# Pooling the first pair's expert tokens by gathering eight rows from a DRAM table

## Chip, cores, metric

The kernel runs on one core of one Trainium2 chip. The metric is the device time of one execution in microseconds. All arithmetic is in float32.

## The reference, cut to what matters

The input is 4 images of 128 channels by 64 x 64, so 4 x 4096 tokens of 128 numbers. Layer 0 adds a full softmax attention between the tokens of an image. Layer 1 adds a running attention with 8 heads to the tokens and then a mixture of 64 experts that choose tokens. This last part is where the change lies:

```
logits = einsum('bsd,ed->bse', x, gate_w) + gate_b     # x: normalised tokens
probs  = softmax(logits, axis=1)                       # over the 4096 tokens
vals, idx = top_k(probs.transpose(0, 2, 1), 8)         # 8 tokens per image and expert
gathered = take_along_axis(x, idx)
pooled   = einsum('bked,bke->bed', gathered, topv)     # weighted sum of the 8 tokens
h   = gelu([pooled, 1] @ weight1);  out = [h, 1] @ weight2
outputs[b, idx] += topv * out                          # back to the 8 tokens
```

## The kernel before

`t` holds all tokens on the chip, 128 tokens by 128 numbers a chunk, four chunks to a block of 512 tokens, 32 blocks in all (8 to an image). Layer 0 runs first and takes the first 1440 us. Then `layer1` runs `loop()` (L1146): one turn n per block, 0 to 31, with the order of PE written out by hand (`tc.manual_schedule`), while a scheduler orders DVE, ACT, POOL (GpSimd) and SP from data dependences and from the `tc.issue_after` pins.

A turn n does this on PE, in this order: the first four key matmuls of block n + 1 (`keys`, L364); the transposes of the score exponentials (`weights`, L910); the transposes of the normalised tokens of block n - 2 for the gate (`gate_turn`, L1036); four more key matmuls; the values (`values`, L946, sixteen records); the gate's logits of block n - 2 (`gate_logits`, L1044); the transposes of the tokens of block n + 2 (`turned`, L354); the running sums (`totals`, L962); the scores of block n + 1 (`score`, L839); the outputs (`outputs`, L985 and L992).

The scores go through `scan`: DVE copies them (L853), takes the running maximum (L858) and subtracts it (L862); ACT takes the exponential (L866); POOL copies the last maximum into `state` (L867) and the exponentials into `es` (L871); DVE sums them (L879) and takes the reciprocal (L884). `spread` sends the reciprocals through DRAM (`rd`) and back, broadcast, as `rb` (L892, L899, on SP's queue). POOL multiplies the exponentials with a mask into `em` (L925), and DVE multiplies `em` with `rb` (L934); `outputs` reads it.

The gate normalises block n - 1 in turn n (`gate_norm`): DVE makes the statistics and the root's reciprocal `grs` (L92), POOL normalises the four chunks into `gate_room` (L96) and copies the roots (L1030). `gate_logits` writes the logits into `lgs[p]`, where p is a pair of images, 0 or 1, and the 128 partitions are 2 images x 64 experts; DVE keeps the eight largest logits of each block in `cand[p]` (L1051).

Once the first pair's 16 blocks have logits, `k0 = n - 18` counts its eight columns of blocks. In turn 18 `select(0)` takes the eight largest logits of the row, `top`, from `cand`. In turns 18 to 25 `pick_exp` (ACT, L1090) and `pick_keep` (DVE, L1100) replace the logits by the exponentials where the logit is at least the eighth largest, and by zero elsewhere. In turns 19 to 26 the pooling follows as dense products: `pick_turn` transposes four chunks of this sparse array on PE (L1111), DVE multiplies them with the roots (`ct`, L1114), and `pick_add` multiplies them with all 1024 tokens of the two blocks on PE (`pick_sum`, L1125) and adds the result to `total` (L1134, L1136). `pick_turn` is pinned ahead of DVE's `weighted` (L934). `total` is used in the tail by `pool_tokens`, which subtracts its mean and divides. The second pair is pooled the same way in the tail, after the loop.

A test at the end counts how many tokens each expert chose (`count`, by ACT's sign function). When a row has more than eight, or a layer 0 sum is out of range, both layers run again in a safer form (`ready` false).

Of the kernel before, what the change touches and what calls it, by code (L numbers as in the profile page):

```python
# [18 lines left out]
def conv_attn_hybrid_kernel(  # L19
# [23 lines left out]
    nc = tc.nc  # L43
    B, C, N = x.shape
    R = w1t.shape[1]
    NH = qt.shape[1]
    E = gwt.shape[1]
# [3 lines left out]
    BLK = 512  # L51
    NBLK = N // BLK
    CPB = BLK // P
# [258 lines left out]
    rows = resid.tile([P, B * NCH], F32, tag="rows", name="rows")  # L312
# [475 lines left out]
    def layer1(pre, ready):  # L788
# [6 lines left out]
        with ExitStack() as kept, ExitStack() as l1:  # L795
# [5 lines left out]
            lgp = pool("lg", side="right")  # L801
            gp = pool("gate", side="right")
# [201 lines left out]
            cand = [lgp.tile([P, NBLK, 8], F32, tag=f"ca{p}", name=f"{pre}ca_{p}") for p in range(B // 2)]  # L1004
            den = lgp.tile([P, B // 2, NBLK], F32, tag="den", name=f"{pre}den")

            count = lgp.tile([P, B // 2, NBLK], F32, tag="count", name=f"{pre}count")
            rden = lgp.tile([P, B // 2], F32, tag="rden", name=f"{pre}rden")

            total = lgp.tile([P, C], F32, tag="total", name=f"{pre}total")  # L1010

            gate_room = gp.tile([P, 2 * BLK], F32, tag="gate_room", name=f"{pre}gate_room")
            gmv, grs, xgs, gate_xts, picks, eighth, cts, lefts = {}, {}, {}, {}, {}, {}, {}, {}

            def gate_stats(n):
                gmv[n] = gp.tile([P, CPB, 2], F32, tag="gmv", name=f"{pre}gmv_{n}", bufs=2)
# [3 lines left out]
            def gate_norm(n, engine):  # L1020
                grs[n] = gp.tile([P, CPB], F32, tag="grs", name=f"{pre}grs_{n}", bufs=2)
                root = roots(grs[n], gmv[n])
                xgs[n] = gate_room[:, :BLK].rearrange("p (c d) -> p c d", c=CPB)
                for c in range(CPB):
                    normalise(
                        engine, xgs[n][:, c, :], n * CPB + c, gmv[n][:, c, 0:1],
                        grs[n][:, c : c + 1],
                    )

                nc.gpsimd.tensor_copy(rs1[:, bass.ts(n, CPB)], grs[n])  # L1030
                return root
# [21 lines left out]
            def select(p):  # L1053

                flat = cand[p].rearrange("p k e -> p (k e)")
                top = gp.tile([P, 8], F32, tag=f"top{p}", name=f"{pre}top_{p}")
                nc.vector.max(out=top, in_=flat)
                ng = gp.tile([P, 1], F32, tag=f"ng{p}", name=f"{pre}ng_{p}")
                i = nc.vector.tensor_scalar_mul(ng, top[:, 0:1], -1.0)
                picks[p], eighth[p] = ng, top[:, 7:8]  # L1060
# [13 lines left out]
                i = nc.vector.tensor_add(flat, flat, sel)  # L1074
                return i.ins
# [54 lines left out]
            def pick_add(p, k):  # L1130
# [4 lines left out]
                else:  # L1135
                    nc.vector.tensor_add(total, total, pp)  # L1136

            def divisors(p):
                nc.vector.tensor_reduce(rden[:, p : p + 1], den[:, p, :], AX.X, ALU.add)
                nc.vector.reciprocal(rden[:, p : p + 1], rden[:, p : p + 1])  # L1140
# [5 lines left out]
            def loop():  # L1146
# [8 lines left out]
                for n in range(NB):  # L1155
# [23 lines left out]
                    with ExitStack() as order:  # L1179
                        if k0 == 0:  # L1180
                            with tc.issue_after(made[2][1]):
                                order.enter_context(tc.issue_after(select(0)))
                        if 0 <= k0 < NBLK:
                            left = gp.tile([P, BLK], F32, tag="left", name=f"{pre}left_0_{k0}")
                            marked = pick_mark(0, k0, left)
                            if marked is not None:
                                order.enter_context(tc.issue_after(marked))
                        if 1 <= k0 <= NBLK:
                            order.enter_context(tc.issue_after(pick_turn(0, k0 - 1, ps_kv)))
                        if k0 == NBLK:  # L1190
                            divisors(0)
                        aas = weighted(ems, rbs)
# [5 lines left out]
                    vs, last = values(n, xt_of[n])  # L1198
                    if n >= 2:
                        best = gate_logits(n - 2, ps_kv)  # L1200
                    if 1 <= k0 <= NBLK:
                        pick_add(0, k0 - 1)
                    with tc.issue_after(last):
                        if n >= 1 and more:
# [11 lines left out]
                    if more:  # L1216
# [360 lines left out]
```

## Time and profile before

| | |
|---|---|
| median of 3 runs (lowest to highest) | 2379.5 us (2378.95 to 2381.96) |
| profiled execution, its own time | 2380.49 us |
| its span, first to last instruction | 2378.7 us |
| TensorE clock granted | 0.997 of full speed |
| PE busy | 2338.3 us, 98% |
| DVE, ACT, POOL busy | 1495.5, 1205.3, 302.9 us |
| L1111, dense transposes, both pairs | 64 records, 10.7 us busy |
| L1125, dense products, both pairs | 256 records, 18.2 us busy |
| L1114, `ct` on DVE, both pairs | 16, 11.0 us busy |
| transfers issued from POOL | none |

A timeline row gives start and duration in microseconds, the engine, the line, the operation, output and inputs by their names, their shapes and how many instructions were merged; a bracket tells how long the engine had stood idle before it and what ended that. PE is TensorE's matmul, PEld its weight load, SPq SyncE's queue. A float32 product leaves two matmul records, a transpose one. An idle engine costs nothing unless what it does next is waited for.

### The profile page before, as it was taken

What the parts mean: (1) busy time and instruction counts of PE and PEld (TensorE: products, weight loads), DVE (VectorE), ACT (ScalarE), POOL (GpSimd) and SP (SyncE); (2) the same over time, 40 slices, a digit from 0 to 9 for tenths busy, and PEclk for the clock granted to TensorE, in tenths of its full rate; (3) what the DMA queues carried; (4) which work ended last, traced back from release to release, by engine and by line L of the source; (5) the groups of instructions that cost most, each with busy time, mean ns of one, the idle gap of its engine ahead of it and who ended that gap; (6) DMA issues with size and microseconds to landing.
All of it is one profiled execution on the core that took longest, in us unless ns stands there. A gap on an engine that the chain in (4) does not pass through costs nothing.

```text
span 2378.7 us, 45711 instructions
## 1 busy us (share of the span) xinstructions
PE 2338.3 (98%) x19416; PEld 1554.5 (65%) x19416; DVE 1495.5 (63%) x2593; ACT 1205.3 (51%) x1637; POOL 302.9 (13%) x338
## 2 busy tenths in 40 slices
PE   7999999999999999999999999999999999999997
PEld 3477777677778677778777775555555555655554
DVE  6666666666656666655555556666666676776655
ACT  5444444444444444443433435666666666666541
POOL 0000000000000000000000001343333343333300
PEclk9999999999999999999999999999999999999999
DMA  3200110001100000020000000212112112112388
GB/s 83 75 23 19 44 37 1 17 13 23 49 25 1 19 12 23 16 54 1 1 1 1 1 1 19 55 38 51 43 38 56 38 44 49 38 38 52 122 307 323
DMA packets 61766, 109.94 MB, mean 46 GB/s; under 512 B 10096, under 2 KB 35184, under 8 KB 61552
## 3 DMA queue, kind: packets, MB, share of 16 engines
q1 hardware_dynamic: 57824, 101.22, 14.9%
q10 hardware_dynamic: 3728, 5.71, 0.7%
q8 instruction: 154, 2.52, 0.5%
q14 instruction: 60, 0.49, 0.1%
HBM read 85.40 MB, written 8.91 MB: 40 GB/s over the span
## 4 chain that ended last, share of the span: by engine, by line


## 5 line engine op out<-in xcount | busy, mean ns | idle before, releaser
L608 PE MATMUL av<-pr,am 64*128 64x512 f32 x4096 | 1057.5, 591 | 0.3 <-ACT pr L587 0.3
L587 ACT ACTIVATE pr<-sc 128x1024 f32<-128x1024 f32 x512 | 523.8, 1023 | 674.5 <-PE sc L583 605.8
L590 DVE TENSOR_TENSOR acc<-acc,pr 128x1024 f32<-128x1024 f32 x480 | 586.9, 1223 | 436.1 <-ACT pr L587 436.0
L608 PEld LDWEIGHTS av<-pr,am 64*128 64x128 f32 x4096 | 634.3, 187 | 260.8 <-issue 40.8
L583 PE MATMUL sc<-e,e 64*128 64x512 f32 x2048 | 617.7, 592 | 1.9 <-DMA e<-ee 1.9
L583 PEld LDWEIGHTS sc<-e,e 64*128 64x128 f32 x2048 | 316.8, 187 | 106.0 <-issue 17.8
L364 PE MATMUL pk<-room,wks 128*128 128x512 f32 x508 | 238.3, 607 | 2.2 <-ACT room L365 1.9
L946 PE MATMUL pv<-wvs,room 128*128 128x512 f32 x512 | 225.4, 593 | 0.5 <-ACT room L365 0.4
L950 ACT ACTIVATE v<-pv 128x512 f32<-128x512 f32 x256 | 152.7, 597 | 72.0 <-PE pv L946 72.0
L934 DVE TENSOR_TENSOR em<-em,rb 128x1024 f32<-128x1024 f32 x64 | 78.4, 1224 | 153.4 <-DMA rb<-rd 153.4
L365 ACT ACTIVATE room<-pk 128x512 f32<-128x512 f32 x254 | 146.8, 597 | 54.5 <-PE pk L364 54.2
L828 POOL MEMSET ew<- 128x1024 f32 x1 | 1.0, 952 | 1360.8 <-PE av L608 1360.8
L946 PEld LDWEIGHTS pv<-wvs,room 128*128 128x128 f32 x512 | 96.3, 190 | 119.1 <-issue 113.7
L364 PEld LDWEIGHTS pk<-room,wks 128*128 128x128 f32 x508 | 89.4, 189 | 107.8 <-issue 79.0
L925 POOL TENSOR_TENSOR em<-et,mask 128x1024 f32<-128x1024 f32 x64 | 122.6, 1936 | 81.3 <-ACT et L912 81.3
L985 PEld LDWEIGHTS po<-v,em 64*64 64x64 f32 x4096 | 113.7, 134 | 28.1 <-DVE before L972 25.1
L96 POOL TENSOR_SCALAR gate_room<-t,gmv,grs 128x128 f32<-128x128 f32 x120 | 95.2, 805 | 281.8 <-DVE grs L92 193.7
L985 PE MATMUL po<-v,em 64*64 64x128 f32 x4096 | 122.3, 273 | 1.8 <-issue 1.8
L884 DVE RECIPROCAL rr<-rr 128x512 f32<-128x512 f32 x32 | 107.3, 3353 | 1.1
L866 ACT ACT_TABLE_LOAD x24 | 30.8, 1283 | 115.8 <-DVE ss L862 115.8
L972 DVE TENSOR_TENSOR before<-before,pt 128x128 f32<-128x128 f32 x256 | 72.7, 284 | 9.7 <-PE pt L962 3.8
L879 DVE TENSOR_TENSOR_SCAN rr<-ones,state,ss 128x512 f32<-128x512 f32 x28 | 42.0, 1500 | 46.6 <-ACT ss L866 46.6
(208 smaller groups left out, 2029.5 us busy)
## 6 DMA issues: line engine op xcount, KB each, us to landing
rb<-rd SPq DMA_DIRECT2D x128, 256.0 KB
fw<-in_fw_dram SPq DMA_DIRECT2D x39, 512.0 KB
room<-in_fw_dram SPq DMA_DIRECT2D x18, 512.0 KB
t<-in_xtok_dram SPq DMA_DIRECT2D x32, 256.0 KB
e<-ee SPq DMA_DIRECT2D x63, 128.0 KB
x<-in_x_dram SPq DMA_DIRECT2D x12, 512.0 KB
e<-ee SPq DMA_DIRECT2D x63, 64.0 KB
out_dram<-t SPq DMA_DIRECT2D x8, 256.0 KB
```

Of the source, the lines that this page charges most:

```text
L96: i = engine.tensor_scalar(out=dst, in0=t[:, chunk, :], scalar1=mean, scalar2=rs, op0=ALU.subtract, op1=ALU.mult)
L364: nc.tensor.matmul(pk, wks[:, h, :], xt, start=True, stop=True)
L365: nc.scalar.activation(kss[h], pk, AF.Silu)
L583: nc.tensor.matmul(sc[:, u, :], e2[halves[u], p, :], e1[halves[u], :], start=True, stop=True)
L587: nc.scalar.activation(pr, sc, AF.Exp)
L590: added.append(nc.vector.tensor_add(acc, acc, pr).ins)
L608: nc.tensor.matmul(av, am[h, j, :], pr[h, u, :], start=(j == 0), stop=(j == NCH - 1))
L884: inverse = nc.vector.reciprocal(rr, rr).ins
L925: nc.gpsimd.tensor_tensor(em, eq.unsqueeze(2).to_broadcast([P, 2 * NH, H2]), mask.unsqueeze(1).to_broadcast([P, 2 * NH, H2]), ALU.mult,)
L946: nc.tensor.matmul(pv.rearrange("p h d -> p (h d)"), xt[:, bass.ts(2 * q + s, P)], wvs[:, bass.ts(m, BLK)], start=True, stop=True,)
L950: last = nc.scalar.activation(v[:, bass.ts(m, HPB), :], pv, AF.Silu).ins
L985: nc.tensor.matmul(po[s * H2 : (s + 1) * H2, u, q, :], aas[q][half, s, h, :], vs[2 * q + s][half, h, :], start=(q == 0 and h == 0), stop=F ...
```

## The change

It acts on the first pair only, and only in the normal run (`ready` true). Each block that `gate_norm` normalises in turns 1 to 16 is also written from `gate_room` to a table `xd` in DRAM, 8192 rows of 128 numbers, by a transfer issued from POOL. In turns 18 to 25 `find` takes, on DVE, the positions of the block column's eight candidates within the block and turns them into row numbers of `xd` (`where`). In turn 26 `gather_chosen` picks, for each of the row's eight largest logits, the row number of the candidate that equals it, and POOL issues eight indirect transfers of 128 rows each from `xd`; equal logits among the eight raise `count` by 100, which makes the end test fail. ACT takes the eight exponentials as `share`. In turn 27 `sum_chosen` adds the eight gathered tokens, each times its share, into `total`. `pick_turn` and `pick_add` are no longer called for the first pair. `pick_exp` and `pick_keep` stay.

```diff
-            count = lgp.tile([P, B // 2, NBLK], F32, tag="count", name=f"{pre}count")
+            count = lgp.tile([P, B // 2, NBLK + 1], F32, tag="count", name=f"{pre}count")
...
+            PAIR = 2 * N
+            if ready:
+                xd = dram.tile([PAIR, C], F32, tag="xd", name=f"{pre}xd", bufs=1)
+
+                row0 = gp.tile([P, 1], F32, tag="row0", name=f"{pre}row0")
+                for z in range(2):
+                    nc.gpsimd.memset(row0[z * E : (z + 1) * E, :], float(z * N))
+                nc.gpsimd.memset(count[:, :, NBLK:], 0.0)
+                where = gp.tile([P, NBLK, 8], F32, tag="where", name=f"{pre}where")
+                rows = gp.tile([P, 8], mybir.dt.uint32, tag="rows", name=f"{pre}rows")
+                share = gp.tile([P, 8], F32, tag="share", name=f"{pre}share")
...
@@ gate_norm, between the normalise and the copy of the roots
+                if ready and n < B // 2 * NBLK:
+                    nc.gpsimd.dma_start(
+                        out=xd[bass.ts(n, BLK), :].rearrange("(c p) d -> p c d", c=CPB), in_=xgs[n]
+                    )
...
+            def find(k):
+
+                at = gp.tile([P, 8], mybir.dt.uint32, tag="at", name=f"{pre}at_{k}")
+                nc.vector.max_index(
+                    out=at, in_max=cand[0][:, k, :], in_values=lgs[0][:, bass.ts(k, BLK)]
+                )
+                nc.vector.tensor_scalar(
+                    out=where[:, k, :], in0=at, scalar1=float(k * BLK), scalar2=row0,
+                    op0=ALU.add, op1=ALU.add,
+                )
+
+            def gather_chosen():
+
+                top = tops[0]
+                same = gp.tile([P, 8], F32, tag="same", name=f"{pre}same")
+                nc.vector.tensor_tensor(same[:, 1:8], top[:, 0:7], top[:, 1:8], ALU.is_equal)
+                nc.vector.tensor_reduce(same[:, 0:1], same[:, 1:8], AX.X, ALU.add)
+                nc.vector.tensor_scalar_mul(count[:, 0, NBLK:], same[:, 0:1], 100.0)
+                rowf = gp.tile([P, 8], F32, tag="rowf", name=f"{pre}rowf")
+                for j in range(8):
+                    hit = gp.tile([P, NBLK * 8], F32, tag="hit", name=f"{pre}hit_{j}")
+                    nc.vector.scalar_tensor_tensor(
+                        out=hit, in0=cand[0].rearrange("p k e -> p (k e)"), scalar=top[:, j : j + 1],
+                        in1=where.rearrange("p k e -> p (k e)"), op0=ALU.is_equal, op1=ALU.mult,
+                    )
+                    nc.vector.tensor_reduce(rowf[:, j : j + 1], hit, AX.X, ALU.add)
+                nc.vector.tensor_scalar(
+                    out=rows, in0=rowf, scalar1=float(PAIR - 1), scalar2=None, op0=ALU.min
+                )
+                got = []
+                for j in range(8):
+                    if j % CPB == 0:
+                        g = gp.tile([P, CPB, C], F32, tag="ct", name=f"{pre}chosen_{j}", bufs=2)
+                    nc.gpsimd.indirect_dma_start(
+                        out=g[:, j % CPB, :], out_offset=None, in_=xd[:, :],
+                        in_offset=bass.IndirectOffsetOnAxis(ap=rows[:, j : j + 1], axis=0),
+                        bounds_check=PAIR - 1, oob_is_err=False,
+                    )
+                    got.append(g[:, j % CPB, :])
+                return got
+
+            def sum_chosen(got):
+                for j, g in enumerate(got):
+                    if j == 0:
+                        nc.vector.tensor_scalar_mul(total, g, share[:, 0:1])
+                    else:
+                        nc.vector.scalar_tensor_tensor(
+                            out=total, in0=g, scalar=share[:, j : j + 1], in1=total,
+                            op0=ALU.mult, op1=ALU.add,
+                        )
...
@@ loop
-                        if 1 <= k0 <= NBLK:
+                        if 1 <= k0 <= NBLK and not ready:
                             order.enter_context(tc.issue_after(pick_turn(0, k0 - 1, ps_kv)))
...
-                    if 1 <= k0 <= NBLK:
+                    if 1 <= k0 <= NBLK and not ready:
                         pick_add(0, k0 - 1)
...
                         if 0 <= k0 < NBLK:
                             with tc.issue_after(made[2][1]):
+                                if ready:
+                                    find(k0)
                                 pick_keep(0, k0)
+                        if ready and k0 == NBLK:
+                            with tc.issue_after(made[2][0]):
+                                nc.scalar.activation(share, tops[0], AF.Exp, bias=picks[0])
+                            with tc.issue_after(made[2][1]):
+                                got = gather_chosen()
+                        if ready and k0 == NBLK + 1:
+                            with tc.issue_after(made[2][1]):
+                                sum_chosen(got)
```

`made[2]` holds the exponential (0) and the reciprocal (1) of the scan of block n + 1. As built, POOL's order in turns 1 to 16 is normalise, roots, write of `xd`, `state`, `es`; in turn 27 it is `em`, the eight gathers, normalise. On DVE, `find` stands behind the reciprocal L884, `gather_chosen` behind that of turn 26 and `sum_chosen` behind that of turn 27.

More of the change, by code (lines that the diff above doesn't have):

```diff
@@ L1012, in layer1 @@
             gate_room = gp.tile([P, 2 * BLK], F32, tag="gate_room", name=f"{pre}gate_room")
+            PAIR = 2 * N
[8 more added lines that the diff above has]
+                share = gp.tile([P, 8], F32, tag="share", name=f"{pre}share")
             gmv, grs, xgs, gate_xts, picks, eighth, cts, lefts = {}, {}, {}, {}, {}, {}, {}, {}
+            tops = {}
             def gate_stats(n):
@@ L1059, in select @@
                 i = nc.vector.tensor_scalar_mul(ng, top[:, 0:1], -1.0)
-                picks[p], eighth[p] = ng, top[:, 7:8]
+                picks[p], eighth[p], tops[p] = ng, top[:, 7:8], top
                 if ready:
```

## The prediction

> **What bounds the kernel now.** I read part 1 of the page first, the engines' busy time.
>
> ```profile
> PE 2338.3 (98%) x19416; PEld 1554.5 (65%) x19416; DVE 1495.5 (63%) x2593; ACT 1205.3 (51%) x1637; POOL 302.9 (13%) x338
> ```
>
> PE is busy 98% of the span, so work taken off PE can shorten the run, but only in the stage where it stood. The removed dense products (L1111, L1125) stand in the loop over blocks, in turns n = 19 to 26. So I read PE's timeline there. I count a body from the first output matmul (L985) of turn n to that of n + 1, so the products of turn 19 lie in body 18:
>
> ```profile
> 1948.23 3.72 PE L985 MATMUL po<-v,em 64*64 64x128 f32 x128
> ...
> 1960.83 0.60 PE L1111 MATMUL ctr<-ident,lg 128*128 128x128 f32 x4
> 1961.27 7.03 PE L946 MATMUL pv<-wvs,room 128*128 128x512 f32 x16
> 1968.14 1.02 PE L1044 MATMUL pl<-gate_room,gws 128*128 128x512 f32 x2
> 1969.09 1.09 PE L1125 MATMUL pp<-t,ct 128*64 128x128 f32 x16
> 1970.11 0.66 PE L354 MATMUL ltr<-ident,room 128*128 128x128 f32 x4
> ...
> 1974.52 3.72 PE L985 MATMUL po<-v,em 64*64 64x128 f32 x128
> ```
>
> Columns: start, duration, engine, line, tiles, count. The body lasts 1974.52 - 1948.23 = 26.29 us and no row carries an idle bracket: PE works without a gap. The same view earlier, where nothing is pooled:
>
> ```profile
> 1549.34 3.72 PE L985 MATMUL po<-v,em 64*64 64x128 f32 x128
> 1553.00 1.09 PE L992 MATMUL po<-before,rr 128*64 128x128 f32 x16
> 1554.02 3.71 PE L364 MATMUL pk<-room,wks 128*128 128x512 f32 x8
> ...
> 1574.02 1.21 PE L985 MATMUL po<-v,em 64*64 64x128 f32 x36
> ```
>
> 24.68 us. Starting every body at L985 through the whole loop: 24.68 for n = 2 to 9, 24.95 for most of n = 10 to 17, 26.28 to 26.35 for the eight with pooling, 25.04 and 24.95 after. PE sets the body's length, except for the 0.27 between 24.68 and 24.95; there the first eight key matmuls (L364) take 3.98 instead of 3.71. What they wait for is seen in one body across engines, the timelines of DVE, ACT and POOL:
>
> ```profile
> 1575.29 1.28 DVE L858 TENSOR_TENSOR_SCAN mm<-ss,state 128x512 f32<-128x512 f32 x1
> 1576.60 0.69 DVE L862 TENSOR_TENSOR ss<-ss,mm 128x512 f32<-128x512 f32 x1
> ```
> ```profile
> 1577.39 1.28 ACT L866 ACT_TABLE_LOAD   x1 [5.12 <-DVE ss L862]
> 1578.69 0.63 ACT L866 ACTIVATE ss<-ss 128x512 f32<-128x512 f32 x1
> 1579.34 1.28 ACT L365 ACT_TABLE_LOAD   x1
> 1580.63 1.61 ACT L365 ACTIVATE room<-pk 128x512 f32<-128x512 f32 x3
> ```
> ```profile
> 1574.95 0.19 POOL L1030 COPY rs<-grs 128x4 f32<-128x4 f32 x1
> 1576.70 0.64 POOL L867 COPY state<-mm 128x1 f32<-128x1 f32 x1 [1.56 <-DVE mm L858]
> 1579.38 1.67 POOL L871 COPY es<-ss 128x256 f32<-128x256 f32 x2 [2.04 <-ACT ss L866]
> ```
>
> Scan and subtraction on DVE, then table, exponential and table on ACT, then three evictions in arrears: PE's fourth key matmul needs the first eviction. This chain has no slack in bodies with two table loads, so a DVE delay here costs PE the same time. In the pooling bodies the exponential's table is already there (L1090 loaded it) and the chain has 1.3 us in hand, which the change keeps.
>
> **What the Trainium skill says.** "DMA: Bandwidth & Descriptors", section "SWDGE vs HWDGE vs iDMA": a transfer issued from GpSimd has its descriptors made in software by two GpSimd cores, so it occupies POOL. No transfer before is issued from POOL; nothing here shows it. "Perfetto Trace Analysis", section "DMA Instruction — SWDGE (GPSIMD)": the profile's window of such an instruction ends with its last descriptor, not with the landing. "SBUF — State Buffer", section "Who interferes with whom": DVE and GpSimd share a port pair as an exclusive lock; a copy on DVE, or an operation with two SBUF inputs against a reading GpSimd operation, blocks or is blocked. This trace agrees: the copy L969 takes 301 ns at least and 1928 beside POOL's products L925. "Vector Engine (DVE) Microarchitecture Reference", section "The match/index hardware and the swap-based sort pattern": finding eight positions is a value load and then a pass over the data, so two instructions.
>
> **The change part by part.**
>
> 1. Removed on PE: 4 transposes (L1111, 1961.27 - 1960.83 = 0.44) and 8 products, recorded as 16 (L1125, 1970.11 - 1969.09 = 1.02), with the joints, since L354 follows L1044 after 0.86 instead of 0.95. In all 26.29 - 24.68 = 1.61 per body, times 8: **-12.9 us**, all on the path. In those bodies the exponential chain keeps its slack, so 24.68 and not 24.95 is what remains. If ACT came in late as in the others, 8 x 1.34 = -10.7.
>
> 2. DVE in those bodies loses ct (0.69) and the add to total (0.29), and gains find: the search, estimated at 0.9 from the MAX8 rows (0.69 over 512, 0.22 over 64), and one small tensor_scalar, 0.16. Net about +0.1. It stands behind the reciprocal L884, ahead of pick_keep, L969 and the add into t, and these now lie wholly beside POOL's L925, which may block them for up to 1.9. Behind them waits the product em (L934):
>
> ```profile
> 1965.01 1.23 DVE L934 TENSOR_TENSOR em<-em,rb 128x1024 f32<-128x1024 f32 x1 [2.73 <-DMA rb<-rd]
> ```
>
> The bracket is idle time until the broadcast lands: 2.73 here, and 4.56 in the body that pools nothing at 2150.28. The cover is that wait, and behind it em's consumer on PE, L985 at 1974.52, six more. Cost 0 (ends 0 and +0.5 each).
>
> 3. POOL gets one write of 256 KB per block (L1043 of the changed file) in bodies 1 to 16, in pieces of 512 bytes, 512 of them. In POOL's order it stands behind rs (ends 1575.14) and ahead of the state copy and es. The exponential waits only for the es copies of the body before, so POOL's delay reaches PE by one way: es, then the transposes L910 at 1582.24. es starts at 1579.38 with the exponential; the state copy takes 0.2 when undisturbed. So the issue is free up to 1579.38 - 1575.14 - 0.64 = 3.6 us, and up to 4.8 without touching PE (es ends 1581.05, 1.2 ahead of L910). No row gives its price. The skill's first page above gives about 1 us to the first byte; if 128 pieces cost that, 512 cost 4 (an estimate), and a lock by DVE could add up to the 2 us of L858 and L862: 1 to 6.5. I take 2.5 to 4, cost 0. The landing (2.0 us + 256 KB at 436 GB/s = 2.6, from the same page, section "Anatomy of one DMA — SWDGE (gpsimd) path") is waited for only by the next body's normalise, 20 us later. The queues that carry rd and rb start 10 us into the body, after it.
>
> 4. Once, in body 26: 20 small DVE instructions (8 products over 64, about 0.23; 8 sums, 0.2; four of 0.16) make about 4.6 us with their joints, before an em that waits 4.56. Cost 0 to 0.5. Then POOL issues 8 gathers, each 128 rows, behind L925 and ahead of the normalise. They start when the rows are known, near 2150.3 on the old clock, and the normalise could start at 2154.8. At 1 us each they end at 2158.3; normalise 3.1 and two copies follow, and es still meets 2163. At 2 us they end at 2166.3 and es ends near 2171.5 against L910 at 2165.83, so PE stands for about 5.7. The normalise then also runs beside the scan. I take 1.3 us each and **+2 us** (ends 0 and +8).
>
> 5. Body 27: 8 scaled adds over 128 (0.35) and three small ones, 3.6 us in another em wait of 4.56; ACT's share (0.2) once. 0. The tail's own pooling of the second pair, SP's order and PE's order otherwise are unchanged.
>
> Sum: -12.9 + 2.0 = -10.9 on the profiled 2380.5 (span 2378.7 and 1.8 around it), 2369.6. The median of the runs stands 1.0 under the profiled one, so **2368.6**.
>
> **The rivals.**
>
> Write issue as the new bound (slower). If one write holds POOL for x us over 4.8, or its lock stops the scan at L858, PE pays it 16 times. Break-even is 10.9 / 16 = 0.68 us per body, so x = 5.5. At 6.5 the cost is 27 and the time 2379.5 - 10.9 + 27 = 2396. For it: the exponential chain is without slack just where the write is issued (1575.2), and 512 pieces are many. Against: DVE is idle from 1577.3 to 1579.35, POOL has 3.6 us to spare, and by the section on ports an operation with two SBUF inputs, as the scan, meets only a GpSimd operation that reads SBUF, while descriptors are written.
>
> Partial loss (about the same). A leak of 0.3 to 1 us in the 16 bodies, or dear gathers with find blocked in each body: 5 to 16 us given back, 2374 to 2384. For it: L969's 1928 ns shows how dear the lock is. Against: the em waits stand behind it.
>
> It doesn't act as said. Equal logits among the eight set the count over its limit, and the second copy of the layer runs: well over 1000 us more. With 4096 float32 values per row that is a matter of one chance in hundreds.
>
> **How the numbers follow.** Forecast 0.65 (2366 to 2374), partial loss 0.14, write-bound 0.20, fallback 0.01. A measurement of this kernel tells 0.2%, 4.8 us, from no change: faster 0.65, same 0.14, slower 0.21. The range starts at 2366 (all of -12.9 and a little) and must reach into the write-bound case, to 2388; about 0.15 lies above. The forecast's own range is 2366 to 2374.
>
> **What would show it.** Bodies n = 18 to 25 at 24.7 us; n = 1 to 17 unchanged, with L364 at 3.71 or 3.98; a POOL row L1043 under 4.8 us; es ending before L910; one longer body, 26 or 27. It is wrong if bodies 1 to 16 grow, if L853, L858 or L862 start later after L985, or if the eight bodies keep more than 25.

## The result and the profile after

| | before | after |
|---|---|---|
| median (lowest to highest), us | 2381.53 (2378.95 to 2382.35), 6 runs | 2370.64 (2369.88 to 2371.56), 6 runs |
| profiled execution, its own time | 2380.49 | 2371.08 |
| its span | 2378.7 | 2369.7 |
| L985 of turn 0 to L985 of turn 31 | 777.40 | 771.26 |
| from there to PE's last instruction | 117.65 | 112.54 |

The ratio of the medians is 0.9957, its 95% interval 0.9944 to 0.9969. The change is faster by 10.9 us, and the interval leaves 7.4 to 13.3. The median before is 2381.53 over six executions; the 2379.5 ahead of the prediction was that of the first three of them. Line numbers below are those of the changed kernel: L1111 became L1128, L1125 became L1142, L1036 L1053, L1044 L1061, L1030 L1047, L1139 L1207.

Part 1 of the page, the same row as before:

```profile
PE 2325.5 (98%) x19256; PEld 1544.9 (65%) x19256; DVE 1514.7 (64%) x2629; ACT 1205.3 (51%) x1638; POOL 322.3 (14%) x365
```

PE lost 160 instructions and 12.8 us, POOL gained 27 instructions and 19.4 us. PE's timeline of body 20, which pooled before:

```profile
1973.48 3.72 PE L985 MATMUL po<-v,em 64*64 64x128 f32 x128
...
1986.08 7.03 PE L946 MATMUL pv<-wvs,room 128*128 128x512 f32 x16
1992.95 1.02 PE L1061 MATMUL pl<-gate_room,gws 128*128 128x512 f32 x2
1993.81 0.60 PE L354 MATMUL ltr<-ident,room 128*128 128x128 f32 x4
...
1998.15 1.10 PE L985 MATMUL po<-v,em 64*64 64x128 f32 x32
```

1998.15 - 1973.48 = 24.67 us; the prediction named 24.7. On DVE in that body the search and the row number stand where ct stood:

```profile
1982.44 0.68 DVE L1158 FIND_INDEX8 at<-ca,lg 128x8 uint32<-128x512 f32 x1
1983.04 1.60 DVE L969 COPY before<-before 128x128 f32<-128x128 f32 x1
1984.57 1.88 DVE L1161 TENSOR_SCALAR where<-at,row 128x8 f32<-128x8 uint32 x1
...
1989.94 1.23 DVE L934 TENSOR_TENSOR em<-em,rb 128x1024 f32<-128x1024 f32 x1 [0.84 <-DMA rb<-rd]
```

em still waits for the broadcast, 0.84 us. In a body that writes a block (4), POOL and then DVE:

```profile
1576.60 0.18 POOL L1047 COPY rs<-grs 128x4 f32<-128x4 f32 x1
1576.94 0.82 POOL L1043 DMA_DIRECT2D xd<-gate_room  x1 [0.16 <-POOL rs L1047]
1578.39 0.70 POOL L867 COPY state<-mm 128x1 f32<-128x1 f32 x1 [0.63 <-DVE mm L858]
```
```profile
1577.04 1.28 DVE L858 TENSOR_TENSOR_SCAN mm<-ss,state 128x512 f32<-128x512 f32 x1
```

The write holds POOL for 0.82 us beside the scan, and neither delays the other: the scan takes its 1.28 us as before. Two bodies show costs. DVE and then PE at the start of body 25 (L985 at 2096.91):

```profile
2097.32 0.16 DVE L1207 TENSOR_REDUCE rden<-den 128x1 f32<-128x8 f32 x1 [1.91 <-ACT left L1107]
...
2099.39 0.41 DVE L853 COPY ss<-ps 128x256 f32<-128x256 f32 x1
```
```profile
2105.15 1.13 PE L364 MATMUL pk<-room,wks 128*128 128x512 f32 x2 [0.72 <-ACT room L365]
```

The sum of divisors waits 1.91 us for ACT, and the scan's copy L853 behind it starts 2.48 us after L985 instead of 0.2. The gathers on POOL, and PE in body 27:

```profile
2142.01 1.89 POOL L1188 DMA_INDIRECT chosen<-xd,rows  x1 [6.02 <-DVE rows L1181]
2144.20 1.02 POOL L1188 DMA_INDIRECT chosen<-xd,rows  x1 [0.30 <-issue]
...
2152.94 1.00 POOL L1188 DMA_INDIRECT chosen<-xd,rows  x1 [0.30 <-issue]
2153.97 3.81 POOL L96 TENSOR_SCALAR gate_room<-t,gmv,grs 128x128 f32<-128x128 f32 x4
...
2158.00 0.73 POOL L871 COPY es<-ss 128x256 f32<-128x256 f32 x2
```
```profile
2158.44 0.77 PE L910 MATMUL pe<-ident,es 128*128 128x128 f32 x4 [2.07 <-POOL es L871]
2159.05 0.72 PE L1053 MATMUL gtr<-ident,gate_room 128*128 128x128 f32 x4
2159.57 5.21 PE L364 MATMUL pk<-room,wks 128*128 128x512 f32 x8
```

Eight gathers take 2153.94 - 2142.01 = 11.93 us, the normalise and es follow, and PE waits 2.07 us for es. The 5.21 us of the key matmuls behind it, against 3.68 in other bodies, have another cause. The trace tells in which stretches TensorE's granted clock was lower. Here is the view of one such stretch, for PE alone:

```profile
core 0: us, PE busy (x), PEclk, DMA share, GB/s
2159.40:2162.80 3.40, 3.40 (x7) 0.50 0.20 47
```

PEclk is the granted clock, here 0.50 of full speed; the columns before it are the stretch, its length and PE's busy time. It is 0.5 from 2159.39 to 2162.81 and full in the rest of this loop.

Where nothing is changed most body lengths repeat to 0.02 us from profile to profile (24.67 to 24.69 for bodies 3 to 9), so bodies tell tenths of a microsecond, which medians cannot. The part after the loop scatters by 5.6 us (112.0 to 117.7) over the fourteen profiles of this study, though PE's work there is the same. The granted clock sorts it. It falls to 0.5 there for 3.41 us at a time, and these profiles take 112.0 to 113.5 us with no such stretch ahead of the last one at the end of the program (five profiles), 114.1 to 114.8 with one (three), 114.9 to 116.2 with two (five) and 117.65 with three (the one profile of the kernel before). One such place, in PE's timeline of the kernel before and then of the one after, the last outputs of the loop:

```profile
2251.83 0.88 PE L985 MATMUL po<-v,em 64*64 64x128 f32 x22
2253.71 4.93 PE L985 MATMUL po<-v,em 64*64 64x128 f32 x106 [0.99 <-issue]
```
```profile
2246.81 4.20 PE L985 MATMUL po<-v,em 64*64 64x128 f32 x128
```

The first took 6.8 us with a gap that nothing released and a clock of 0.5 from 2253.93 to 2257.34, the second 4.2. The 2.6 us are part of the difference of the two spans. It is not the mark of the change: kernels with the change have up to two such stretches after the loop. What brings a stretch about was not tested.

### The profile page after: what moved, and what is told of

It reads as the page before. It is cut to its first block, busy times and chain, and to the rows that moved or that the text cites. A ratio compares the mean times of both kernels' runs of the same rounds, so it can differ in the third digit from the quotient of the medians.

```text
span 2369.7 us, 45400 instructions
## 1 busy us (share of the span) xinstructions
PE 2325.5 (98%) x19256; PEld 1544.9 (65%) x19256; DVE 1514.7 (64%) x2629; ACT 1205.3 (51%) x1638; POOL 322.3 (14%) x365
## 4 chain that ended last, share of the span: by engine, by line
## 5 line engine op out<-in xcount | busy, mean ns | idle before, releaser
L364 PE MATMUL pk<-room,wks 128*128 128x512 f32 x508 | 240.0, 610 | 3.5 <-ACT room L365 3.4
L934 DVE TENSOR_TENSOR em<-em,rb 128x1024 f32<-128x1024 f32 x64 | 78.3, 1224 | 132.2 <-DMA rb<-rd 130.7
L364 PEld LDWEIGHTS pk<-room,wks 128*128 128x128 f32 x508 | 90.1, 191 | 110.3 <-issue 79.2
L985 PEld LDWEIGHTS po<-v,em 64*64 64x64 f32 x4096 | 112.1, 133 | 26.6 <-DVE before L972 24.3
L985 PE MATMUL po<-v,em 64*64 64x128 f32 x4096 | 120.7, 271 | 0.3
L884 DVE RECIPROCAL rr<-rr 128x512 f32<-128x512 f32 x32 | 107.3, 3353 | 1.1
L879 DVE TENSOR_TENSOR_SCAN rr<-ones,state,ss 128x512 f32<-128x512 f32 x28 | 42.1, 1502 | 46.6 <-ACT ss L866 46.6
```

The source lines that it names most:

```text
L364: nc.tensor.matmul(pk, wks[:, h, :], xt, start=True, stop=True)
L884: inverse = nc.vector.reciprocal(rr, rr).ins
L985: nc.tensor.matmul(po[s * H2 : (s + 1) * H2, u, q, :], aas[q][half, s, h, :], vs[2 * q + s][half, h, :], start=(q == 0 and h == 0), stop=F ...
```

## The experiments

All edits are against the changed kernel. "Loop" is L985 of turn 0 to L985 of turn 31 in the profile; the kernel before has 777.40.

| run | median, us | its before | loop, us | body 25, 26, 27, 28 |
|---|---|---|---|---|
| after | 2370.64 | 2381.53 | 771.26 | 25.66, 25.37, 28.74, 24.95 |
| 1 products out | 2368.44 | 2379.16 | 765.61 | 25.66, 24.95, 24.96, 24.95 |
| 2 no gathers | 2367.59 | 2379.16 | 766.01 | 25.66, 25.14, 24.95, 24.95 |
| 3 sum later | 2368.96 | 2379.16 | 768.11 | 25.67, 25.38, 27.03, 24.95 |
| 4 divisors later | 2370.70 | 2379.16 | 767.39 | 24.67, 25.38, 27.05, 24.95 |
| 5 gathers in 28 | 2369.78 | 2379.78 | 770.20 | 25.67, 25.27, 29.75, 24.67 |
| 6 both | 2368.80 | 2379.78 | 768.59 | 24.67, 25.14, 28.09, 24.67 |
| 7 four writes | 2377.62 | 2379.78 | 777.76 | 25.68, 36.61, 24.67, 24.96 |
| 8 eight writes | 2378.26 | 2379.78 | 777.74 | 25.67, 36.67, 24.67, 24.95 |
| 9 four writes, no gathers | 2367.72 | 2380.04 | 765.64 | 25.67, 25.14, 24.95, 24.95 |
| 10 probe of eight | 2378.26 | 2380.04 | 777.19 | 25.67, 25.37, 27.05, 24.95 |
| 11 probe of four | 2377.08 | 2380.04 | 773.97 | 25.67, 25.48, 27.05, 24.95 |
| 12 four and four | 2366.42 | 2379.32 | 765.33 | 24.67, 25.14, 24.95, 25.47 |

The intervals of the ratios reach about 3 us to either side of each median's difference, so the verdicts below rest on bodies and rows.

### 1. Only the products out

```diff
-                if ready and n < B // 2 * NBLK:
-                    nc.gpsimd.dma_start(
...
-                                if ready:
-                                    find(k0)
...
-                                got = gather_chosen()
...
-                                sum_chosen(got)
+                                nc.vector.memset(total, 0.0)
```

> Only the removal: the dense products of the first pair are gone and nothing takes their place (no table, no find, no gathers; the first pair's pooled sum is set to zero, so that part of the result is left out). My theory: the replacement costs the kernel only two things on the path, the longer body 27 (+3.8 us, behind the gathers) and about 0.3 in body 26, so this kernel stands 4 us under the changed one, near 2366.5, with body 27 back at 24.95 and body 26 at 25.0; body 25 keeps its extra 1.0 because the sum of divisors (rden) still stands ahead of the scan there. Rival 1 (the 16 writes and the eight searches cost something as well, spread thin): 6 to 10 us under the changed kernel, with bodies 1 to 16 shorter than in it. Rival 2 (the extra of body 27 has nothing to do with the replacement): within 1 us of the changed kernel. The last body and the tail are about 4 us shorter in the one profile of the changed kernel than in that of the kernel before; if that is a lasting gain of the missing products, it is here too, if chance, it is not.

Bodies 18 to 24 at 24.67 to 24.71, body 25 at 25.66, 26 and 27 at 24.95 and 24.96: the bodies are as expected. The sizes are not: the loop is 5.7 us under that of the changed kernel and the median 2.2, where I expected 4. The 16 writes cost nothing in bodies 3 to 9, which are 24.67 to 24.68 with and without them. And the 1.0 us of body 25 belongs to the removal itself: the transposes' pin is gone with them.

### 2. No gathers

```diff
-                    nc.gpsimd.indirect_dma_start(
-                        out=g[:, j % CPB, :], out_offset=None, in_=xd[:, :],
...
-                                sum_chosen(got)
+                                nc.vector.memset(total, 0.0)
```

> Everything of the change but the eight gathers and the sum over them (the first pair's pooled sum is set to zero, so that part of the result is left out): the 16 writes, the searches, the row numbers stay. My theory, the gathers' 11.9 us on POOL ahead of the normalise make body 27 long: body 27 falls from 28.7 to 24.95, the time by 3.8, to 2366.8, within 0.5 us of the kernel with the products only taken out. Rival (the 20 small operations on DVE, or the writes, delay what PE waits for): body 27 or 26 stays over 26 and the time falls by less than 1.5.

Body 27 falls to 24.95, and the loop lies 0.4 us from run 1. So the extra of body 27 comes from the gathers. The searches, the row numbers and the writes together cost 0.4, most of it in two bodies: 0.28 in body 19 (24.99 against 24.71) and 0.19 in body 26 (25.14 against 24.95).

### 3. The sum a turn later, and the gathers where they were

```diff
-                                got = gather_chosen()
-                        if ready and k0 == NBLK + 1:
+                                gather_chosen()
+                        if ready and k0 == NBLK + 2:
...
+                    if ready and k0 == NBLK + 1:
+                        with tc.issue_after(masked[n]):
+                            got = gather_rows()
```

> The eight gathers are issued one turn later, right behind the mask products on POOL, with their row numbers long there, and the sum one turn later still. My theory: POOL is idle for about 9 us there (mask products end 11.3 after L985, the normalise starts 20.3 after it), the gathers take 10.4 to 11.9, so the normalise comes 1.5 to 3 us late instead of 8.9 us, es still makes its time, and no body is longer than 25.4: 3.5 us under the changed kernel, near 2367. Rival (gathers slow the transfers of rb or block DVE wherever they stand): the body in which they are issued stays over 27.5 and the time within 1.5 us of the changed kernel.

The edit missed its aim. The mask products of turn 27 are issued in body 26, ahead of the row numbers, and the gathers kept their place on POOL; only the sum moved. That makes it a repeat of the changed kernel with other details the same. PE in body 27:

```profile
2156.30 0.78 PE L910 MATMUL pe<-ident,es 128*128 128x128 f32 x4 [2.07 <-POOL es L871]
2156.91 0.60 PE L1053 MATMUL gtr<-ident,gate_room 128*128 128x128 f32 x4
2157.35 3.60 PE L364 MATMUL pk<-room,wks 128*128 128x512 f32 x8
```

The wait is the same 2.07 and the second four key matmuls take 3.60 instead of 5.21. So of the 3.8 in the changed kernel's body 27, 2.1 is the gathers' wait, which returns in runs 3, 4, 10 and 11, and 1.7 is the stretch at half the clock, which of these profiles only that of the changed kernel has there.

### 4. The divisors pinned later

```diff
-                        if k0 == NBLK:
+                        if k0 == NBLK and not ready:
                             divisors(0)
...
+                        if ready and k0 == NBLK + 2:
+                            with tc.issue_after(made[2][1]):
+                                divisors(0)
```

> One thing only: the sum of divisors and its reciprocal (divisors of the first pair) are pinned two turns later, behind the reciprocal L884. In the changed kernel they lost the pin that the dense products' transposes gave them and stand ahead of the scan's copies L853, where they wait 1.9 us for ACT. My theory: body 25 falls from 25.66 to 24.67, the time by 1.0, to 2369.6, if body 27 stays at 28.7. Rival (L853 is late for another reason, such as the tenth of a search or a late score): body 25 stays at 25.6 and the time does not move.

Body 25 is 24.67. DVE's timeline there (L985 at 2094.85):

```profile
2093.28 1.87 DVE L972 TENSOR_TENSOR before<-before,pt 128x128 f32<-128x128 f32 x6
2095.06 0.42 DVE L853 COPY ss<-ps 128x256 f32<-128x256 f32 x1
```

L853 starts 0.21 after L985 again. The median did not show the 1.0 us, the body did.

### 5. The gathers in turn 28

```diff
-                    if ready and k0 == NBLK + 1:
+                    if ready and k0 == NBLK + 2:
                         with tc.issue_after(masked[n]):
                             got = gather_rows()
```

(against run 3, and the sum in turn 29)

> The eight gathers are issued behind the mask products of turn 28, not 27, and the sum over them in turn 29; the divisors stay where the change put them. This is the move that the run with the sum one turn later did not make, since its gathers kept their place. My theory: POOL is idle there for 9.0 us (mask products end 13.4 us after L985, the normalise starts 22.4 after it) and the row numbers are long known, so the gathers (10.4 to 11.9 us) make the normalise at most 2.9 us late, es still makes its time 5.4 us after the next L985, and no PE instruction waits: body 27 and body 28 at 24.95, body 26 stays at 25.38, the loop 2.1 us shorter than with the gathers in their old place. Rival (gathers cost PE 2 us wherever they stand, by blocking DVE or the broadcast's transfers): 2 us move from body 27 to body 28.

The wait of L910 for es is gone, as expected, but body 27 is 29.75, not 24.95: the running sums L962 take 5.75 us there instead of 1.96, in pieces with gaps that nothing releases, and the scores behind them 2.86 instead of 1.85, at a granted clock of 0.5 from 2172.13 to 2175.54. My theory of a pure POOL delay does not hold. Nor does the rival: body 28 is 24.67.

### 6. Both moves

The edits of runs 4 and 5 together.

> Both repairs together: the gathers in turn 28 and the divisors pinned two turns later. My theory: the two add up, 2.1 and 1.0 us less in the loop; body 25 at 24.67, body 26 at 25.38, bodies 27 and 28 at 24.95, the loop from L985 of turn 0 to that of turn 31 at 765.3 us against 777.4 before, and the time 3 us under the changed kernel, near 2367.5, 12 under the one before. Rival (what is late next takes the place, such as the search's operations ahead of em): body 25 or 28 over 25.3 and the loop at 766.5 or more.

Body 25 is repaired, body 27 is 28.09, L962 5.09 in it, and the clock stays full. The loop of 768.59 lies in the rival's range, but not for the rival's reason: bodies 25 and 28 are 24.67 both, and the loss is in L962.

### 7 and 8. Four and eight writes a block

```diff
+                spare = [
+                    dram.tile([PAIR, C], F32, tag=f"xd{i}", name=f"{pre}xd{i}", bufs=1)
+                    for i in range(7)
+                ]
...
-                    nc.gpsimd.dma_start(
-                        out=xd[bass.ts(n, BLK), :].rearrange("(c p) d -> p c d", c=CPB), in_=xgs[n]
-                    )
+                    for table in (*spare, xd):
+                        nc.gpsimd.dma_start(
+                            out=table[bass.ts(n, BLK), :].rearrange("(c p) d -> p c d", c=CPB),
+                            in_=xgs[n],
+                        )
```

(three spare tables for four writes)

> Each block is written four times from POOL instead of once, to four tables. The prediction held the write issue free up to 3.6 us of POOL and without effect on PE up to 4.8. At 0.82 each and 0 to 0.3 between them, four take 3.3 to 4.2 us. My theory: bodies 1 to 16 unchanged (24.68 and 24.95), the time within 1 us of the changed kernel. Rival (the slack is smaller, since the scan's exclusive port or the state copy stands in between, or the tables' transfers delay the broadcast): bodies 3 to 9 longer by 0.3 or more, the time 5 us or more longer.

> Each block is written eight times from POOL, to eight tables. Eight take 6.6 to 8.7 us of POOL, which is 1.8 to 3.9 over the 4.8 that the prediction held to be without effect. My theory: PE waits at L910 for es in bodies 1 to 16, each 1.8 to 3.9 us longer, the time 29 to 62 us longer than the changed kernel, 2400 to 2433: the rival of the prediction, made true. Rival (POOL's issue lies off the path altogether, or only the transfers count): bodies unchanged, or em waits longer for its broadcast instead of L910 for es.

Bodies 3 to 17 are unchanged with four and with eight. POOL in body 4 of run 8, and PE:

```profile
1576.59 6.04 POOL L1048 DMA_DIRECT2D xd<-gate_room  x8 [0.16 <-POOL rs L1053]
1582.63 0.20 POOL L867 COPY state<-mm 128x1 f32<-128x1 f32 x1
1582.75 0.74 POOL L871 COPY es<-ss 128x256 f32<-128x256 f32 x2
```
```profile
1583.81 0.60 PE L910 MATMUL pe<-ident,es 128*128 128x128 f32 x4
```

Eight issues take 6.04 us, 0.755 each, and es ends at 1583.49, 0.32 ahead of L910. The slack is 6.04 + 0.32 = 6.4 us and not 4.8: es takes 1.67 us where it stands beside DVE's sum L879, and 0.74 here, where it comes later. My expectation for eight failed in these bodies. Body 1 alone shows how near the bound is. The eight issues start 2.8 us after L985 there instead of 1.0, and PE has the wait that I expected; the body takes 26.15 us, against 25.38 with four writes and 24.97 to 25.46 with one:

```profile
1509.70 0.77 PE L910 MATMUL pe<-ident,es 128*128 128x128 f32 x4 [0.92 <-POOL es L871]
```

Both runs show something else: 36.6 us in body 26, and medians of twelve executions that are only 2.2 and 1.5 us under their kernel before. PE's timeline there in run 7:

```profile
2142.30 1.28 PE L962 MATMUL pt<-v,ew 64*32 64x128 f32 x49
2143.89 0.43 PE L962 MATMUL pt<-v,ew 64*32 64x128 f32 x3 [0.32 <-issue]
2144.66 0.39 PE L962 MATMUL pt<-v,ew 64*32 64x128 f32 x3 [0.34 <-issue]
...
2152.71 1.57 PE L962 MATMUL pt<-v,ew 64*32 64x128 f32 x43 [0.78 <-issue]
```

PE issues a few of these short products, three on the mean (41 in 9.6 us), each 0.74 us. It waits for no engine and no transfer that the profile shows. On POOL in the same run the gathers stand from 2140.42 to 2151.46. The granted clock does not start this: it is full until 2147.06, 4 us into the stall, and then 0.5 until 2157.30. What the clock costs shows best behind the stall, where the scores L839 take 3.36 us instead of 1.85. Run 8 is alike (0.5 from 2148.09 to 2158.33, scores 3.48).

### 9. Four writes, no gathers

The edit of run 2 on the kernel of run 7.

> The kernel with four writes a block, without the eight gathers and their sum (the first pair's pooled sum is set to zero, so that part of the result is left out). With the gathers its body 26 took 36.6 us instead of 25.4, all of it in gaps in PE's own issue inside the running sums L962, while the gathers were issued. Theory 1: the gathers starve PE's instruction supply; the writes are only what came before. Then body 26 is 25.1 here and the time 11 to 12 us shorter than with them, near 2367. Theory 2: the many writes do it (64 instead of 16 have gone through POOL's queue by then): body 26 stays over 30 without the gathers.

Body 26 is 25.14, L962 1.96. Without the gathers there is no stall, with four writes a block as before; eight writes without gathers were not run.

### 10 and 11. A probe of eight or four gathers a turn

```diff
+                    if ready and 4 <= n <= 17:
+                        with tc.issue_after(masked[n]):
+                            for j in range(8):
...
+                                nc.gpsimd.indirect_dma_start(
+                                    out=g[:, j % CPB, :], out_offset=None, in_=probe["tab"][:, :],
+                                    in_offset=bass.IndirectOffsetOnAxis(
+                                        ap=probe["rows"][:, j : j + 1], axis=0
+                                    ),
+                                    bounds_check=BLK - 1, oob_is_err=False,
+                                )
```

> The changed kernel with a probe: in turns 4 to 17 POOL issues eight more gathers of 128 rows each behind the mask products, from a small table of its own, into a tile that nothing reads. Mask products end 13.0 us after L985, L962 starts 20.9 after it, so eight gathers (10.4 to 11.9 us) run on into L962 and the next L985. Theory 1, gathers in flight beside L962 or L985 starve PE's issue: many of the bodies 3 to 16 grow, by 1 to 11 us each and unevenly, with gaps without a releaser in L962. Theory 2, the cost is only POOL's delay of the normalise and of es: the normalise is at most 2.9 us late, the slack covers it, and bodies 3 to 16 stay at 24.68 and 24.95; the long bodies seen so far came by chance.

> The same probe with four gathers a turn. They are issued from 13.1 to 18.3 us after L985 and have landed by 20.8, while PE works on the long value products L946, which need few instructions, and before L962 starts at 20.9. Theory 1 (starved issue beside L962): bodies 3 to 16 stay at 24.68 and 24.95, or grow by under 0.3. Theory 3 (any gather beside PE costs PE time, in proportion): each of these bodies grows by half of what eight gathers cost it.

The length of L962, from its first product to the first score, sorts all runs:

| gathers and L962 | bodies | L962, us |
|---|---|---|
| none issued beside it (all runs, the probe of four too) | all others of bodies 0 to 28 in 14 profiles | 1.96 |
| eight, the tail of them beside it (run 10) | 14 | 2.04 to 2.46 |
| the real eight, in body 26 (after, 3, 4, 10, 11) | 5 | 2.18 to 2.20 |
| the real eight, in body 27 (5, 6) | 2 | 5.75, 5.09 |
| the real eight, in body 26 after 64 and 128 writes (7, 8) | 2 | 11.92, 11.88 |

L962 is longer in every body where POOL issues gathers beside it and in none where it does not. In bodies 11 and 13 of the probe of four the last gathered packets end up to 0.6 us after L962 has begun, and it stays at 1.96. Theory 1 holds for where the time goes, not for its size: I expected 1 to 11 us a body, and L962 grew by 0.1 to 0.5 in fourteen overlaps, with 3 to 10 us only in runs 5 to 8. And that PE's instruction supply is what starves is argued, not shown.

The probe of four leaves L962 alone and still adds 0 to 1.25 us to these bodies, 0.27 on the mean. It shows in the first key matmuls L364: the second em starts 20.3 to 22.4 us after L985 (bodies 3 to 15) where the kernel before has 19.7 to 20.8. em waits for the broadcast rb. Counted from the end of the reciprocals, which are sent, the second em starts 10.17 us later on the mean of bodies 3 to 16 with the probe of four and 9.62 in the kernel before, so the broadcast arrives 0.55 later; all that DVE does behind em, the scan's copies among it, starts later too. The eight writes of run 8 do not do that (9.39). Eight gathers cost 0.49 on the mean, 0.26 of it in L962; the other 0.23 is no more than four cost. So the totals stand in the proportion of theory 3, though the rows show two places for the time and not one.

### 12. Four gathers in turn 28 and four in 29

```diff
-                    if ready and k0 == NBLK + 2:
+                    if ready and k0 in (NBLK + 2, NBLK + 3):
                         with tc.issue_after(masked[n]):
-                            got = gather_rows()
+                            if k0 == NBLK + 2:
+                                got = gather_rows(range(4))
+                            else:
+                                got += gather_rows(range(4, 8))
```

(against run 6, and the sum in turn 30)

> The version that the runs point to: four gathers behind the mask products of turn 28 and four behind those of turn 29, the sum in turn 30, the divisors pinned two turns later. Four gathers behind the mask products end before L962 and cost 0 to 1.25 us, 0.27 on the mean of fourteen bodies, through the later broadcast. My theory: no gap in PE's issue, body 25 at 24.67, bodies 27 and 28 together at most 1 us over 49.9, the loop from turn 0 to turn 31 at 765.3 to 766.5 us, 1 to 2 under the version with the gathers in their old place and the divisors moved, the time near 2367.5. Rival (gathers from the large table stall PE's issue wherever they stand after turn 27): body 27 or 28 over 27 and the loop over 767.5.

POOL and PE in body 27:

```profile
2157.90 1.14 POOL L1190 DMA_INDIRECT chosen<-xd,rows  x1 [0.16 <-issue]
...
2161.97 1.00 POOL L1190 DMA_INDIRECT chosen<-xd,rows  x1 [0.30 <-issue]
```
```profile
2165.66 2.03 PE L962 MATMUL pt<-v,ew 64*32 64x128 f32 x128
```

The fourth is issued by 2162.97, while PE is on the value products. L962 takes 2.03 again (1.96 to the first score). Bodies 25 to 28 are 24.67, 25.14, 24.95 and 25.47, and the loop is 765.33, 12.1 us under the kernel before and 0.3 under the kernel with the products only taken out, which still has its divisors early. The median is 12.9 under its own before (ratio 0.9945, 0.9932 to 0.9959). It is the best of the runs; against the changed kernel the intervals overlap, and the loop decides.

## Why the prediction was right, and where it was not

The predicted 2368.6 stands against 2370.64, and the predicted difference of 10.9 against one of 10.9; the 2.0 between the times is the median before, which six executions put at 2381.53 instead of 2379.5. By the loop the change itself is worth less. The changed kernel's own profile has 6.1 us under before, about 7.8 without its stretch at half the clock, and run 3, the changed kernel but for the sum, has 768.11, which is 9.3 under before. So the equal tenths are luck, within an interval of 7.4 to 13.3; what was right is the mechanism, the products' time coming back in their bodies and the gathers' delay of es.

Step 1, products on PE. Right: 24.67 in most of the bodies, -1.62 each, where 1.61 was predicted. The eighth, body 25, first gave only -0.63. With the divisors moved (run 4) it gives 1.62, and the eight bodies together 12.8, so that 8 x 1.61 = 12.9 is confirmed. **What was missed** is a pin. `divisors(0)` stood under the pin behind `pick_turn`'s ct, and with `pick_turn` gone it slid ahead of L853 and waited for ACT: +1.0 us. I had followed what the removed code computed, not what was ordered behind it.

Step 2, find. Cost 0 confirmed within 0.4 (runs 1 and 2), together with the row numbers. It is not quite nothing: body 19 is 24.71 in run 1, which has neither searches nor writes, and 24.89 to 25.25 in the twelve kernels that have both. The search took 0.71 with its value load, less than the 0.9; the small tensor_scalar took 1.88, not 0.16, beside POOL's mask products, within the bound of 1.9. em's wait for rb, 2.73 in the body shown of before, is 0.84 in that shown of after, and was not used up.

Step 3, write issue. Cost 0 confirmed, on a wrong size: 0.82 us where I took 2.5 to 4 from an estimate. The rival built on it, the write as the new bound, fails on both sides: the price is a seventh of its break-even of 5.5, and the break-even was too low, since 6.04 us were still free (run 8). The term that failed is the fixed 1.67 for es. The landing, 3.3 us after the issue (median of 16), came later than the estimated 2.6, and nothing waited for it.

Step 4, gathers. +2 predicted by a normalise that delays es and L910, and 2.07 found, by just that chain. The size is partly luck. With 1.3 us a gather the prediction's own figures give 2150.3 + 10.4 for the last issue, then 3.1 for the normalise, 0.4 for two copies and 1.67 for es, which ends at 2165.9, where L910 stands at 2165.83: a wait of nearly nothing, so the +2 was more than its working gave. Measured, the start came 19.4 us after L985 instead of 18.0, with DVE's first two small operations at 0.98 and 2.00 us beside the mask products; the pitch was 1.49 us, not 1.3: 1.0 each, 0.30 between, and two of 1.9; and the normalise took 3.81 beside the scan. The shorter es, 0.73, gave part of that back. Body 26 grew by 0.3, within 0 to 0.5, but not for the 20 small operations alone: with them and without gathers (run 2) it is 25.14, without both (run 1) 24.95, so 0.2 is theirs and another 0.2 comes with the gathers, in L962. What the trace of before could not show is the second way by which gathers cost PE, through its own issue. The changed kernel paid 0.2 for it, by its place; runs 5 to 8 paid 3 to 10.

Step 5, the sum. 0 confirmed: body 27 is 27.05 with the sum in it (run 4) and 27.03 without (run 3).

The ledger of run 3: -12.9 for the products, +1.0 divisors, +0.3 body 26, +2.1 body 27, and 0.2 more in body 19, which comes with the searches or the writes: -9.3.

The lock, as the Trainium skill has it ("SBUF — State Buffer", section "Who interferes with whom": a DVE instruction with two SBUF inputs contends with a GpSimd instruction that reads SBUF, and not with one that only writes it), agrees with both transfers. The write L1043 keeps its 0.82 beside the scan L858; the first gather, issued beside em's product L934, and the sixth, beside L858, took 1.9 instead of 1.0. In run 10 the 26 gathers issued beside em's product took 0.99 to 2.05, the one beside L858 1.94, and all others 0.99 to 1.13. That the gather's reading of its row numbers is what meets the lock is argued, not shown.

**Open**: why PE's issue falls to a few products each 0.74 us beside gathers in some programs (11.9 us for L962 in runs 7 and 8, over twelve executions by their medians) and hardly in others, where the gathers begin at the same place (19.4 us after L985 in the changed kernel and in runs 3, 4, 7 and 8). Where it comes, gathers are being issued, and in runs 5 to 8 it ends 0.5 to 1.3 us after the last issue; what else it needs was not found. The trace has a DMA queue of the kind instruction, and it does not show PE waiting for it: in run 7 the next packet of that queue starts at 2153.70, 1 us after PE has picked up its pace, and run 9, which has no stall, also has its packet near the end of L962.

## What to carry to other kernels

When an edit removes an instruction that others were pinned behind, look up where they go: here a pair of small operations cost 1.0 us by moving ahead of a chain without slack. Price transfers from a software queue where they hold their engine (0.8 us for 512 pieces, 1.3 to 1.5 for 128 gathered rows), and put gathers beside PE work with few and long instructions, in portions that end before the dense part. When medians scatter by 3 us, compare the lengths of repeated bodies, which here repeat to 0.02, and read the granted clock of the stretch before you look for a cause in the program: 1.7 us of body 27 and most of the scatter after the loop go with the clock.

## What the runs showed of the hardware that was not expected

- Beside the issue of gathers, PE's issue of short products slows or stalls without a releaser: L962 takes 1.96 us in every body read without them, 2.04 to 11.92 in every body with them.
- The granted clock falls to 0.5 for 3.41 us (10.24 in runs 7 and 8) in single stretches of a run whose mean is 0.997. In bodies 0 to 29 it did so in four of fourteen profiles, each time after PE had waited or issued slowly (2.07 us of waiting ahead of 2159.39 in the changed kernel; the stalls of runs 5, 7 and 8). The same wait in runs 3, 4, 10 and 11 and the stall of run 6 brought no such stretch.
- A write of 256 KB in 512 pieces, issued from POOL, holds it 0.82 us, eight in a row 0.755 each; an indirect transfer of 128 rows 1.0, and 1.9 when it is issued beside em's product or the scan L858 on DVE, which have two SBUF inputs.
- With four gathers of 64 KB in a body, the product that waits for the broadcast of the reciprocals starts 0.55 us later on the mean, counted from their end (10.17 and 9.62 in bodies 3 to 16), with the transfer engines busy 26% of the stretch from 1580 to 1890 us (19% before).
